# The head of a four-layer kernel: identity by way of DRAM, earlier loads, later roots

## The chip, the cores and the metric

The kernel runs on one core of a Trainium2 chip. The metric is the device time of one launch in microseconds (us). A core has five engines with a queue of instructions each: PE (TensorE, matmul), DVE (VectorE), ACT (ScalarE), POOL (GpSimd) and SP (SyncE, which here only issues DMAs). DMAs can be issued from SP, ACT and POOL.

## The reference, cut to what matters

x is 1 x 256 x 256 x 128 in float32: 65,536 tokens of 128 channels, 33.6 MB. Four layers follow, each `x = x + f(_gn(x))`, where `_gn` is a group norm over all tokens in 32 groups of 4 channels. The change lies in the first layer alone:

```python
x = x + _L0_conv_ref(_gn(x), mask, ln_w, ln_b, w_tri, w_q, w_k, w_v, w_g, b_g, w_o, b_o)

# in _L0_conv_ref, a triangle attention along rows:
mu = mean(x, axis=-1); var = mean((x - mu) ** 2, axis=-1)
xn = (x - mu) * rsqrt(var + EPS) * ln_w + ln_b
tri_bias = einsum('bijd,dh->bhij', xn, w_tri)
q, k, v = xn @ w_q, xn @ w_k, xn @ w_v          # 4 heads of 32
scores = q k^T / sqrt(32) + tri_bias + mask_bias
o = sigmoid(xn @ w_g + b_g) * (softmax(scores) @ v)
return o @ w_o + b_o
```

Two facts of it matter. The group norm needs the mean and variance of all of x before anything after it can start. And the attention adds `tri_bias` of all token pairs to every row's scores, so the per-token mean and variance, and four products with `w_tri`, are needed for all tokens before the first row of attention.

## The kernel before

The work of layer 0 is laid out in two passes over x and a loop of attention. Inside them the order of instructions on each engine is the order of the program (`tc.manual_schedule()`); the constants ahead of them are placed by a scheduler.

**Constants (lines 71 to 168).** `ident`, the 128 x 128 identity that PE's transposes use, is made on POOL by `make_identity`: a memset and an affine_select, an instruction that keeps or replaces elements by their place. Two more block constants are made on POOL with two affine_selects each: `cen16` (its tile is named f1_c, 1/16 on blocks of 16) and `gmat` (1/4 on blocks of 4, the group norm's groups). Then comes `load_library` (line 98), which loads a library of POOL functions, and some fifty DMAs of weights, all issued from POOL (`column` and `weight`, lines 102 to 112, and the lines after). `w_o` is the fifth of them. `woh` (line 432) is a scaled copy of it made on DVE; the scheduler puts it among the instructions of the first pass.

**First pass (lines 257 to 379).** x is read in 32 pieces (`NSC`) of 2048 tokens, 1 MB each, in the order `order0`. `load0(i)` issues the load of piece i from SP into one of three buffers (tag "xt"). Per piece PE transposes sixteen 128 x 128 blocks (line 360) into PSUM tiles of half a piece, of which there are three; DVE takes `bn_stats` of them (line 362); ACT copies them out as channels x tokens (line 367). The first 18 pieces go back to DRAM as `xT` from three buffers of tag "xs" (line 373); the last 14 (`HELD`) stay on chip, in tiles that the attention uses later. From the seventh piece on, one step of `folds()` (weights folded with the norms) comes with each piece. The loads:

```python
for s in range(3):
    load0(s)
mk = ...; nc.sync.dma_start(mk, mask)      # line 353
for i, s in enumerate(order0):
    ...                                    # transposes, bn_stats, copies
    load0(i + 3)
    if s not in held:
        nc.sync.dma_start(xT[...], xc)     # line 373
```

[...]

**Between the passes (lines 401 to 433)** the statistics are merged into the group norm's mean and scale, on which all that follows depends.

**Second pass (lines 436 to 602).** Per piece: ACT squares the normed piece (`p_sq`, line 450); PE multiplies the piece with `wt` (rows1, line 453) and sums the squares (squares1, line 461); DVE evacuates them to `p_tr` (line 466); PE turns them (turn1, line 474); DVE puts them into `raw` (keep1, line 478). Iteration i runs rows1(i), turn1(i-2), squares1(i-1), keep1(i-2). When all pieces of a range are in `raw`, `deviation` makes the variance on DVE (three instructions a range) and its root on ACT (line 487), and `normal`, an iteration later, the reciprocal and the scaling of the products with `w_tri` (lines 492 to 494, DVE). This comes at iterations 9, 17, 24 and 29, the second to fourth with two ranges each, and for the last four pieces after the loop. Some first work of the attention is mixed in: `first_rows` at iteration 11, `first_qk` at 26, `first_v` at 27.

**Attention and the rest (from line 606)** are not touched. DVE's statistics tiles come from the pool `stats_pool` with two buffers, used in turn by the layers.

Of the kernel before, what the change touches and what calls it, by code (L numbers as in the profile page):

```python
# [32 lines left out]
def kernel(ctx: ExitStack, tc: tile.TileContext, a: dict, out: bass.AP):  # L33
# [41 lines left out]
    make_identity(nc, ident)  # L75
# [6 lines left out]
    nc.gpsimd.memset(cen16, -1.0 / 16)  # L82
    for sign, base in ((1, 0), (-1, 15)):
        nc.gpsimd.affine_select(
            out=cen16, in_=cen16, compare_op=ALU.is_ge, fill=0.0, base=base,
            pattern=[[-16 * sign, 8], [0, 16]], channel_multiplier=sign,
        )
    cen16 = cen16.rearrange("p q c -> p (q c)")
    nc.vector.tensor_tensor(cen16, cen16, ident, ALU.add)
    gmat = const.tile([P, 32, 4], F32, name="gmat")  # L90
    nc.gpsimd.memset(gmat, 0.25)
    for sign, base in ((1, 0), (-1, 3)):
        nc.gpsimd.affine_select(
            out=gmat, in_=gmat, compare_op=ALU.is_ge, fill=0.0, base=base,
            pattern=[[-4 * sign, 32], [0, 4]], channel_multiplier=sign,
        )
# [114 lines left out]
    stats_pool = ctx.enter_context(tc.tile_pool(name="stats", bufs=2, reuse_waits="tile"))  # L211

    def new_stats(name):
        return stats_pool.tile([P, T // CK, 6], F32, name=name, tag="gn_stats")

# [41 lines left out]
    with tc.tile_pool(name="x0", bufs=1, reuse_waits="tile") as xres, tc.tile_pool(name="p0", bufs=3, reuse_waits="tile") as sb:  # L257
        tags = [("x", X_BUFS)] * 5 + [("xn", 2)] * 2 + [("rs", 1)]
        held = {s: tuple(gt_tile(f"x0_{s}_{h}", *tags[2 * s + h]) for h in range(2)) for s in range(4)}
        for s in range(4, 9):  # L260
            held[s] = att_sb.tile([P, 2, GT], F32, name=f"x0_{s}", tag="qk" if s < 6 else "vg", bufs=2 if s < 6 else 3)
            held[s] = held[s].rearrange("p a t -> p (a t)")
        for s in range(9, HELD):
            held[s] = xres.tile([P, SC], F32, name=f"x0_{s}")
        order0 = [*range(HELD + FRESH, NSC), *range(HELD, HELD + FRESH), *range(HELD)]
        with tc.tile_pool(name="p0ps", bufs=3, space=PSUM, reuse_waits="tile") as ps, tc.tile_pool(name="f0ps", bufs=2, space=PSUM, reuse_waits="tile") as fps, tc.tile_pool(name="f0", bufs=1, reuse_waits="tile") as wk, tc.manual_schedule():
            xts, loaded = {}, {}

            def load0(i):

                if i < NSC:
                    s = order0[i]
                    xts[s] = sb.tile([P, 2, 8, D], F32, name="p0_x", tag="xt")
                    nc.sync.dma_start(
                        xts[s], x_tok[s * SC : (s + 1) * SC, :].rearrange("(c p k) d -> p c k d", p=P, k=8)
                    )
# [73 lines left out]
            for s in range(3):  # L350
                load0(s)
            mk = wk.tile([P, 2, N], F32, name="mk")
            nc.sync.dma_start(mk, a["L0_conv_mask"].rearrange("b (t p) n -> p (b t) n", p=P))
            for i, s in enumerate(order0):
                xt = xts.pop(s)
                xc = held[s] if s in held else sb.tile([P, SC], F32, name="p0_xc", tag="xs")
                for c in range(2):
                    pt = ps.tile([P, 8, P], F32, name="p0_t")
                    for k in range(8):
                        nc.tensor.transpose(pt[:, k, :], xt[:, c, k, :], ident)  # L360
                    for h in range(2):
                        nc.vector.bn_stats(
                            stats0[:, i * 4 + 2 * c + h, :],
                            pt[:, 4 * h : 4 * h + 4, :].rearrange("p k n -> p (k n)"),
                        )
                    xh = xc[c] if isinstance(xc, tuple) else xc[:, c * GT : (c + 1) * GT]
                    nc.scalar.copy(
                        xh.rearrange("p (n k) -> p n k", k=8),
                        pt.rearrange("p k n -> p n k"),
                    )  # L370
                load0(i + 3)
                if s not in held:
# [62 lines left out]
        with tc.tile_pool(name="p1", bufs=3, reuse_waits="tile") as wk_sb, tc.tile_pool(name="p1ps", bufs=3, space=PSUM, reuse_waits="tile") as ps, tc.tile_pool(name="p1pt", bufs=2, space=PSUM, reuse_waits="tile") as psT, tc.tile_pool(name="p1mm", bufs=3, space=PSUM, reuse_waits="tile") as psP:  # L435
# [7 lines left out]
            with tc.manual_schedule():  # L443
# [38 lines left out]
                def deviation(lo, hi):  # L482
# [3 lines left out]
                    nc.vector.tensor_scalar(var, var, 0.0, None, ALU.max)  # L486
                    nc.scalar.activation(var, var, AF.Sqrt, bias=epst)
# [63 lines left out]
                qscale = 1.0 / float(HC) ** 0.5  # L551
                for i in range(NSC + 2):
# [12 lines left out]
                    if i == 9:  # L565
                        deviation(0, 4)
                    if i == 10:
                        normal(0, 4)
                    if i == 11:
                        first_rows()  # L570
                    if i == 17:
                        deviation(4, 8)
                        deviation(14, 21)
                    if i == 18:
                        normal(4, 8)
                        normal(14, 21)
# [6 lines left out]
                    if i == 24:  # L583
                        load_rs(1)
                        deviation(8, 12)
                        deviation(21, 25)
                    if i == 25:
                        normal(8, 12)
                        normal(21, 25)
# [5 lines left out]
                    if i == 29:  # L595
                        deviation(12, 14)
                        deviation(25, 28)
                    if i == 30:
                        normal(12, 14)
                        normal(25, 28)  # L600
                deviation(28, NSC)
                normal(28, NSC)
# [1423 lines left out]
```

## Time and profile before

| | us |
|---|---|
| median of 3 runs | 3259.66 (3257.19 to 3260.97) |
| the profiled execution | 3258.13 |
| its span, first to last instruction | 3256.4 |
| first pass with the group norm, from the start | 155 |
| second pass | 95 |
| attention, about | 1180 |

Over the span PE is busy 3052.1 us (94%), DVE 2264.2 (70%), ACT 2030.0 (62%) and POOL 1725.2 (53%). The shares differ by stage: in the first 155 us PE is busy 90.5 us, DVE 94.8, ACT 67.4 and POOL 40.7, and the DMA engines have a share of 0.96; in the second pass PE is busy 89.9 of 95 us, and the DMA share is 0.77.

In the profile's timeline a line gives start and duration in us, the engine, the line of the kernel, the operation and its operands (names with numbers left out: `p_x` is a piece of x, `p_pr`, `p_tr` and `p_pt` the second pass's products, their evacuation and their turned form), and in brackets how long the engine had been idle and what ended the wait. "issue" means that it waited for nothing that the profile shows. SPq is SP's queue, PEld PE's weight loads.

### The profile page before, as it was taken

The page shows a single profiled execution, that of the slowest core. Times are in us where ns is not written, and L with a number is a line of the kernel's source. Part 1 is how long each engine was busy: PE and PEld are TensorE (multiplying, and loading weights), DVE is VectorE, ACT ScalarE, POOL GpSimd, SP SyncE. Part 2 cuts the span into 40 slices and gives each one's busy share as a digit, 9 for nine tenths or more (in the row PEclk, how much of TensorE's full clock was granted, in tenths as well). Part 3 has the DMA queues.
Part 4 walks back from the last instruction along what each step waited for, and adds up shares of the span by engine and source line. Part 5 has one row for each costly group of instructions (what it writes and reads, how often), then busy time and mean ns, then how long its engine had stood idle before and what let it go on. Part 6 is the DMA issues. An engine that isn't in the chain of part 4 may idle for free. (4 is left out here: it accounts for less than half of the span.)

```text
span 3256.4 us, 51714 instructions
## 1 busy us (share of the span) xinstructions
PE 3052.1 (94%) x19908; PEld 1634.6 (50%) x19908; DVE 2264.2 (70%) x2617; ACT 2030.0 (62%) x2272; POOL 1725.2 (53%) x925
## 2 busy tenths in 40 slices
PE   5699999999999999996799799999999989979998
PEld 4535555555555555552533344444699933324444
DVE  5657888888888888883546455454455588858887
ACT  3577777777777777754467545444344457757776
POOL 5005777777777777760268000000255568848887
PEclk8899999999999999998899899999999999989999
DMA  9972333333333333339679677666699989986775
GB/s 353 412 299 95 107 124 112 105 125 112 105 124 113 105 123 114 105 134 392 220 305 413 238 275 306 250 253 259 262 351 353 346 316 388 389 290 195 235 231 153
DMA packets 291220, 748.13 MB, mean 230 GB/s; under 512 B 68441, under 2 KB 138731, under 8 KB 242171
## 3 DMA queue, kind: packets, MB, share of 16 engines
q1 hardware_dynamic: 282065, 731.02, 61.6%
q0 software_dynamic: 6064, 12.21, 1.0%
q8 instruction: 160, 2.62, 0.3%
q10 hardware_dynamic: 2840, 1.54, 0.2%
q14 instruction: 91, 0.75, 0.1%
HBM read 457.29 MB, written 287.38 MB: 229 GB/s over the span
## 5 line engine op out<-in xcount | busy, mean ns | idle before, releaser
L680 POOL TENSOR_TENSOR p_es<-p_e 128x1024 f32<-128x1024 f32 x256 | 603.3, 2367 | 304.7 <-ACT p_e L678 234.8
L670 DVE TENSOR_TENSOR p_e<-p_S,tri_raw 128x1024 f32<-128x1024 f32 x512 | 609.2, 1212 | 144.3 <-PE p_S L660 144.2
L678 ACT ACTIVATE p_e<-p_e,mbT 128x1024 f32<-128x1024 f32 x512 | 551.9, 1138 | 62.0 <-DVE p_e L670 62.0
L1231 PE MATMUL p_pm<-p_zn,wf 128*128 128x512 f32 x1040 | 448.7, 593 | 1.9 <-ACT p_a L1266 1.9
L645 PE MATMUL p_mm<-p_xn,w 128*128 128x512 f32 x764 | 404.7, 613 | 0.1
L1231 PEld LDWEIGHTS p_pm<-p_zn,wf 128*128 128x128 f32 x1040 | 196.8, 190 | 253.9 <-issue 246.6
L660 PE MATMUL p_S<-p_qk 32*128 32x256 f32 x4096 | 295.8, 401 | 3.3 <-DVE p_e L670 3.3
L1328 POOL MEMSET k<- 128x512 f32 x1 | 0.5, 525 | 522.4 <-PE p_pm L1231 522.4
L660 PEld LDWEIGHTS p_S<-p_qk 32*128 32x128 f32 x4096 | 186.2, 184 | 159.3 <-PE p_mm L636 91.7
L1984 PE MATMUL tp_z<-p_B,tp_at 128*128 128x256 f32 x1024 | 250.7, 388 | 0.8 <-DMA p_B<-bD 0.6
L693 PE MATMUL p_o<-p_e,p_vg 128*32 128x256 f32 x4096 | 249.2, 384 | 0.0
L627 POOL TENSOR_TENSOR p_xn<-p_xn,p_rs 128x1024 f32<-128x1024 f32 x62 | 148.8, 2400 | 182.5 <-ACT p_xn L622 97.9
L1359 POOL TENSOR_TENSOR k<-k,p_sq 128x512 f32<-128x512 f32 x128 | 163.3, 1276 | 136.0 <-ACT p_sq L1357 136.0
L1984 PEld LDWEIGHTS tp_z<-p_B,tp_at 128*128 128x128 f32 x1024 | 185.1, 190 | 21.8 <-DVE tp_at L1975 1.6
L645 PEld LDWEIGHTS p_mm<-p_xn,w 128*128 128x128 f32 x764 | 125.3, 191 | 104.1 <-issue 88.3
L1358 DVE TENSOR_TENSOR k<-tp_z,k 128x512 f32<-128x512 f32 x128 | 88.5, 692 | 127.0 <-ACT p_sq L1357 127.0
L693 PEld LDWEIGHTS p_o<-p_e,p_vg 128*32 128x32 f32 x4096 | 120.5, 110 | 110.0 <-ACT p_vg L651 41.5
L651 ACT ACTIVATE p_vg<-p_mm,bgh 128x512 f32<-128x512 f32 x128 | 88.0, 687 | 135.5 <-PE p_mm L645 135.5
L1355 ACT COPY p_K<-tp_z 128x512 f32<-128x512 f32 x128 | 75.0, 586 | 155.2 <-PE tp_z L1984 155.2
L1270 DVE SCALAR_TENSOR_TENSOR p_b<-p_pm,b2w,p_b 128x1024 f32<-128x1024 f32 x64 | 82.1, 1284 | 122.2 <-PE p_pm L1231 107.8
L636 PEld LDWEIGHTS p_mm<-w,p_xn 128*128 128x128 f32 x1016 | 134.2, 192 | 61.3 <-issue 60.6
L649 ACT ACTIVATE p_qk<-p_mm,cqkg 128x512 f32<-128x512 f32 x127 | 87.3, 687 | 122.5 <-PE p_mm L645 122.1
(394 smaller groups left out, 6068.6 us busy)
## 6 DMA issues: line engine op xcount, KB each, us to landing
p_x<-x2T SPq DMA_DIRECT2D x60, 1024.0 KB
x<-x1T SPq DMA_DIRECT2D x51, 1024.0 KB
p_x<-in_x_dram SPq DMA_DIRECT2D x32, 1024.0 KB
p_x<-xT SPq DMA_DIRECT2D x64, 512.0 KB
p_rs<-rsD SPq DMA_DIRECT2D x64, 512.0 KB
x2T<-x SPq DMA_DIRECT2D x32, 1024.0 KB
aD<-p_a SPq DMA_DIRECT2D x32, 1024.0 KB
bD<-p_b SPq DMA_DIRECT2D x32, 1024.0 KB
```

What stands on the lines that cost most here:

```text
L627: nc.gpsimd.tensor_tensor(xn, xn, groups[g]["rs"], ALU.mult)
L636: nc.tensor.matmul(pm[:, k * D : (k + 1) * D], lhsT=t["xn"][:, b * P : (b + 1) * P], rhs=wf[:, 2 * D : 3 * D], start=True, stop=True,)
L645: nc.tensor.matmul(pm, lhsT=w, rhs=t["xn"][:, cs_], start=True, stop=True)
L660: nc.tensor.matmul(Ss[h // 2][:, h % 2, u, :], lhsT=t["k"][hp, r * N + u * P : r * N + (u + 1) * P], rhs=t["q"][hp, r * N : (r + 1) * N], ...
L670: nc.vector.tensor_tensor(e[:, :, 2 * p : 2 * p + 2, :].rearrange("p u h n -> p h u n"), Ss[p], triT[:, 2 * p : 2 * p + 2, :, :], ALU.add,)
L678: nc.scalar.activation(e[:, u, :, :], e[:, u, :, :], AF.Exp, bias=mbT[:, u, i : i + 1])
L680: nc.gpsimd.tensor_tensor(es, e[:, 0, :, :], e[:, 1, :, :], ALU.add)
L693: nc.tensor.matmul(t["o"][hp, r % 2, :], lhsT=t["v"][:, r * 2 + u, hp], rhs=e[:, u, h, :], start=(u == 0), stop=(u == 1),)
L1231: nc.tensor.matmul(pm[:, c, :], lhsT=wf2[:, i, :], rhs=zns[s][:, k * CK : (k + 1) * CK], start=True, stop=True)
L1358: nc.vector.tensor_tensor(k1, pz, k1, ALU.add)
L1359: nc.gpsimd.tensor_tensor(k2, k2, sq, ALU.add)
L1984: nc.tensor.matmul(pz[:, t, :], lhsT=at[:, u, t * P : (t + 1) * P], rhs=Bc[:, u, :], start=(u == 0), stop=(u == 1))
```

## The change

- `ident` comes from a diagonal written through DRAM. DVE fills a 128 x 129 tile, `seed`, with zeros and its first column with ones; ACT's queue writes it to `diagD` in DRAM and reads the first 128 x 128 elements back in rows of 128, so that each one lands a place further on. `stats_pool` is made earlier, and `seed` takes a buffer of it.
- `cen16` and `gmat` come from `ident` on DVE: a reduction over blocks and a multiplication of its broadcast. POOL no longer has an affine_select. [...]
- Six pieces of x are asked for ahead of the mask. The fourth to sixth go into the three buffers of tag "vg", which the held pieces 6 to 8 take later; the tiles of the held pieces are therefore made when they are needed. `load0(i + 6)` follows pieces 0 to 2, nothing follows pieces 3 to 5, and `load0(i + 3)` follows the later ones.
- `deviation` is split into `variance` and `root`; root comes an iteration after variance, and normal an iteration after root. For the first range variance starts an iteration earlier, so that its normal stays where it was.
- In the order that the scheduler makes, `woh` moves on DVE from behind the sixteenth `bn_stats` of the first pass to behind the sixth.

```diff
-    make_identity(nc, ident)
+    stats_pool = ctx.enter_context(tc.tile_pool(name="stats", bufs=2, reuse_waits="tile"))
...
+    diagD = dram.tile([P, P + 1], F32, name="diagD")
+    seed = new_stats("seed").rearrange("p n s -> p (n s)")[:, 0 : P + 1]
+    nc.vector.memset(seed, 0.0)
+    nc.vector.memset(seed[:, 0:1], 1.0)
+    nc.scalar.dma_start(diagD, seed)
+    nc.scalar.dma_start(ident, diagD.rearrange("p n -> (p n)")[0 : P * P].rearrange("(p n) -> p n", n=P))
...
-    nc.gpsimd.memset(cen16, -1.0 / 16)
-    for sign, base in ((1, 0), (-1, 15)):
-        nc.gpsimd.affine_select(
-            out=cen16, in_=cen16, compare_op=ALU.is_ge, fill=0.0, base=base,
-            pattern=[[-16 * sign, 8], [0, 16]], channel_multiplier=sign,
-        )
+    gmat = const.tile([P, 32, 4], F32, name="gmat")
+    blocks = const.tile([P, 32], F32, name="blocks")
+    for m, w, value in ((cen16, 16, -1.0 / 16), (gmat, 4, 0.25)):
+        block = blocks[:, 0 : P // w]
+        nc.vector.tensor_reduce(block, ident.rearrange("p (a b) -> p a b", b=w), AX.X, ALU.add)
+        nc.vector.tensor_scalar(m, block.unsqueeze(2).to_broadcast([P, P // w, w]), value, None, ALU.mult)
...
-    gmat = const.tile([P, 32, 4], F32, name="gmat")
-    nc.gpsimd.memset(gmat, 0.25)
-    for sign, base in ((1, 0), (-1, 3)):
-        nc.gpsimd.affine_select(
-            out=gmat, in_=gmat, compare_op=ALU.is_ge, fill=0.0, base=base,
-            pattern=[[-4 * sign, 32], [0, 4]], channel_multiplier=sign,
-        )
...
                 if i < NSC:
                     s = order0[i]
-                    xts[s] = sb.tile([P, 2, 8, D], F32, name="p0_x", tag="xt")
+                    if 3 <= i < 6:
+                        xts[s] = att_sb.tile([P, 2, 8, D], F32, name="p0_x", tag="vg", bufs=3)
+                    else:
+                        xts[s] = sb.tile([P, 2, 8, D], F32, name="p0_x", tag="xt")
...
-            for s in range(3):
-                load0(s)
+            for i in range(6):
+                load0(i)
...
-                xc = held[s] if s in held else sb.tile([P, SC], F32, name="p0_xc", tag="xs")
+                xc = hold(s) if s < HELD else sb.tile([P, SC], F32, name="p0_xc", tag="xs")
...
-                load0(i + 3)
+                if i < 3:
+                    load0(i + 6)
+                elif i > 5:
+                    load0(i + 3)
...
-                def deviation(lo, hi):
+                def variance(lo, hi):
...
+                def root(lo, hi):
+                    var = rsT[:, :, 8 * lo : 8 * hi]
                     nc.scalar.activation(var, var, AF.Sqrt, bias=epst)
...
+                marks = {8: [(0, 4)], 17: [(4, 8), (14, 21)], 24: [(8, 12), (21, 25)], 29: [(12, 14), (25, 28)]}
...
+                    for at, spans_ in marks.items():
+                        for k, step in enumerate((variance, root, normal)):
+                            if i == at + k:
+                                for lo, hi in spans_:
+                                    step(lo, hi)
```

The calls of `deviation` and `normal` at fixed iterations go, and after the loop the three steps run in turn for the last range.

More of the change, by code (lines that the diff above doesn't have):

```diff
@@ L6 @@
 from concourse import library_config, mybir
-from concourse.masks import make_identity
 from concourse._compat import with_exitstack
@@ L74, with new_stats @@
     ident = const.tile([P, P], F32, name="ident")
-    make_identity(nc, ident)
+    stats_pool = ctx.enter_context(tc.tile_pool(name="stats", bufs=2, reuse_waits="tile"))
+    def new_stats(name):
+        return stats_pool.tile([P, T // CK, 6], F32, name=name, tag="gn_stats")
+    diagD = dram.tile([P, P + 1], F32, name="diagD")
[4 more added lines that the diff above has]
+    nc.scalar.dma_start(ident, diagD.rearrange("p n -> (p n)")[0 : P * P].rearrange("(p n) -> p n", n=P))
     ones = const.tile([P, P], F32, name="ones")
@@ L209, in gn_groups @@
         return mean, rstd
-    stats_pool = ctx.enter_context(tc.tile_pool(name="stats", bufs=2, reuse_waits="tile"))
-    def new_stats(name):
-        return stats_pool.tile([P, T // CK, 6], F32, name=name, tag="gn_stats")
     stats0 = new_stats("stats0")
@@ L258, with hold @@
         tags = [("x", X_BUFS)] * 5 + [("xn", 2)] * 2 + [("rs", 1)]
[L259 to L264, printed above, removed]
+        held = {}
+        def hold(s):
+            if s < 4:
+                held[s] = tuple(gt_tile(f"x0_{s}_{h}", *tags[2 * s + h]) for h in range(2))
+            elif s < 9:
+                tile_ = att_sb.tile([P, 2, GT], F32, name=f"x0_{s}", tag="qk" if s < 6 else "vg", bufs=2 if s < 6 else 3)
+                held[s] = tile_.rearrange("p a t -> p (a t)")
+            else:
+                held[s] = xres.tile([P, SC], F32, name=f"x0_{s}")
+            return held[s]
         order0 = [*range(HELD + FRESH, NSC), *range(HELD, HELD + FRESH), *range(HELD)]
@@ L272, in load0 @@
                     s = order0[i]
-                    xts[s] = sb.tile([P, 2, 8, D], F32, name="p0_x", tag="xt")
+                    if 3 <= i < 6:
+                        xts[s] = att_sb.tile([P, 2, 8, D], F32, name="p0_x", tag="vg", bufs=3)
+                    else:
+                        xts[s] = sb.tile([P, 2, 8, D], F32, name="p0_x", tag="xt")
                     nc.sync.dma_start(
@@ L564 @@
                         keep1(i - 2)
[L565 to L568, printed above, removed]
+                    for at, spans_ in marks.items():
[3 more added lines that the diff above has]
+                                    step(lo, hi)
                     if i == 11:
                         first_rows()
[L571 to L576, printed above, removed]
                     if i == 20:
@@ L584 @@
                         load_rs(1)
[L585 to L589, printed above, removed]
                     if i == 26:
@@ L594 @@
                         first_v()
[L595 to L602, printed above, removed]
+                for step in (variance, root, normal):
+                    step(28, NSC)
     stats1 = new_stats("stats1")
```

## The prediction

> **What bounds the kernel now.** The change touches the first 250 us alone, so I read the page's row of DMA shares by fortieths, then windows over that stretch, then the timeline at its two ends. The page's chain stops after one step here and says nothing. Windows (columns: length, busy us of PE, PEld, DVE, ACT, POOL with instructions, granted clock, DMA share, GB/s):
>
> ```profile
> 2.00:11.00 9.00, 0.00 (x0) 0.00 (x0) 0.00 (x0) 0.00 (x0) 0.00 (x0) 1.00 0.98 368
> 11.00:17.00 6.00, 4.22 (x24) 3.98 (x24) 4.29 (x14) 1.05 (x1) 2.16 (x7) 1.00 0.10 17
> 17.00:28.00 11.00, 5.11 (x40) 4.29 (x40) 7.34 (x13) 8.15 (x9) 4.69 (x9) 1.00 0.92 315
> 28.00:118.00 90.00, 57.08 (x312) 50.61 (x312) 49.21 (x93) 33.23 (x33) 33.35 (x64) 0.72 1.02 415
> 118.00:146.00 28.00, 21.03 (x160) 17.18 (x161) 25.94 (x42) 21.04 (x21) 0.00 (x0) 1.00 1.01 391
> ```
>
> See that from 28 us to the arrival of the last piece of x at 146 us the DMA engines are full while PE, ACT and POOL have slack: this first pass over x (32 pieces read, 18 written back) is set by bytes. DVE, at 25.94 of 28 us, is near the bound only at its end. The one place where DMA stands still is 11 to 17 us. The timeline at the head says why:
>
> ```profile
> 0.96 0.21 POOL L77 MEMSET ones<- 128x128 f32 x1
> 12.05 0.28 POOL masks.py:199 TENSOR_SCALAR_AFFINE_SELECT ident<-ident 128x128 f32<-128x128 f32 x1 [10.88 <-issue]
> ...
> 12.39 4.22 PE L360 MATMUL p_t<-ident,p_x 128*128 128x128 f32 x24 [12.39 <-POOL ident masks.py:199]
> ...
> 15.77 0.37 SPq L274 DMA_DIRECT2D p_x<-in_x_dram  x1
> ...
> 19.32 0.86 POOL L111 DMA_DIRECT2D L_conv_ln_w_sb<-in_L_conv_ln_w_dram  x1 [5.11 <-issue]
> ...
> 29.37 0.23 DVE L432 TENSOR_SCALAR woh<-L_conv_w_o_sb 128x128 f32<-128x128 f32 x1 [3.85 <-DMA L_conv_w_o_sb<-in_L_conv_w_o_dram]
> ```
>
> POOL stands 10.88 us before its first affine_select, PE waits for ident until 12.39, only then is an x buffer freed, and the fourth load goes out at 15.77. Three loads and the mask (3.4 MB) last to 11 us. POOL stands another 5.11 us before the first weight DMA.
>
> In the second pass (155 to 250 us) PE runs one iteration per 2.53 us; the starts of its groups of squares (L461) show where it is held. Timeline at the second range:
>
> ```profile
> 202.38 0.35 ACT L487 ACTIVATE tri_raw<-tri_raw,epst 128x64 f32<-128x64 f32 x1 [4.39 <-DVE tri_raw L486]
> ...
> 205.54 1.06 PE L461 MATMUL p_pr<-p_sq,slide 128*32 128x512 f32 x8 [0.75 <-ACT p_sq L450]
> ...
> 207.62 0.74 DVE L466 TENSOR_SCALAR p_tr<-p_pr,off 128x512 f32<-128x512 f32 x1
> ...
> 208.42 0.66 PE L474 MATMUL p_pt<-ident,p_tr 128*128 128x128 f32 x4 [0.96 <-DVE p_tr L466]
> ```
>
> ACT waits for the variance in front of its root, its next Square is late, and PE waits 0.75 us; one iteration on, PE waits for DVE, which is inside the normals.
>
> [...] The two POOL gaps, 10.88 and 5.11 us, [...] the built program has a library reload at each (library 0 ahead of the first affine_select, library 10 at load_library). [...] This stage's queue rows give the upper one: POOL's small transfers landed 4.9 to 8.3 us after issue under full load. [...]
>
> **The change, part by part.**
>
> 1. *Identity.* Removed: one memset, one affine_select and the reload of library 0. Added: two DVE memsets (0.2 and 0.06 us by their neighbours), and two dependent DMAs on ACT's queue, which is idle until 15.95 us. Memsets end near 1.6 us; an issue takes about 0.4 us (0.37 in SP's row). [...] two at 8.3 us give 19. I take 4.5 us a hop[...]: ident near 11 us. Their bytes, 0.13 MB at 0.41 MB/us, cost 0.35 us of a full DMA.
>
> 2. *Constants.* POOL loses two memsets and four affine_selects (2.1 us); DVE gains two reduces (0.18 each) and two multiplies (0.35 each), 1.1 us, between ident and the first bn_stats. Bytes hide it; were DMA not full, it would delay the pass by 1.1 us.
>
> 3. *POOL's start.* Only library 10 is reloaded, from about 1.2 us. Call this reload R: 5.1 us (its own gap) to 10.9 us (the gap under full DMA). First weight DMA at 1.2+R; w_o landed 10.05 us after the first one (29.37 − 19.32), so at 11.25+R: 16.4 to 22.1 us. This matters because woh moves forward in DVE's order, from behind 16 bn_stats to behind six, and everything on DVE queues behind its wait for w_o.
>
> 4. *Six pieces asked for first.* Three loads move ahead of the mask on SP, three more after pieces 0, 1 and 2, none after pieces 3 to 5; 32 loads as before. Six loads, mask and diagonal are 6.69 MB: DMA is busy from 2.0 to 18.3 us. Load 6 needs PE through piece 0, ident + 2.3 us, and some 1.2 us to reach the engines: no gap while ident is there by about 14 us. If DVE is stuck at woh, SP stands at the store of piece 1, behind load 7: eight loads, store 0, mask and diagonal (9.83 MB) keep DMA busy to 26.0 us. Store 1 reaches the engines some 3.5 us after w_o lands (its bn_stats 1.25, copy 1.01, issue and start). So no gap while w_o lands by 22.5 us, R below 11.2.
>
>    Gain: the hole (in windows of one us the idle shares from 10 to 18 us sum to 6.0 us), plus half of the 0.88 us missing in 17 to 28 us (0.08 of 11), minus 0.35: **6.1 us**. Everything behind hangs on the group norm at the pass's end, so it goes through to the end.
>
> 5. *Roots an iteration later.* ACT's wait for the variance goes; no instruction is added. What is late next is DVE. Its iterations 9, 17, 24 and 29 hold the four roots. Intervals of L461 above 2.53 us: at 9, 0.04 (ACT); at 17: 0.81 (ACT) and 0.94 (DVE); at 24: 0.79 (ACT); at 29: 0.52 (ACT). At 17 the two normals are 3.54 us of DVE (204.16 to 207.70) and by themselves put the next p_tr 4.29 us after the last instead of 2.53: 1.76 us, exactly the sum that ACT and DVE cost now, so nothing is won. At 24 the normals fall into the iteration of first_qk and first_v, whose 1.98 and 1.16 us of PE cover DVE: 0.79 won. At 29 they (2.1 us) now stand before the last p_tr and hold it 0.4 us: 0.1 won. Sum **0.8 us**, bounds 0 and 2.2 (all four ACT waits).
>
> Sum: 6.9 us. The profiled execution was 3258.13 us (span 3256.4 and 1.7 around it) and becomes 3251.2; the median of the runs, 3259.66, is 1.5 above it, so I forecast 3252.8.
>
> **The rivals.** 0.2% is 6.5 us, about what a measurement of this kernel can tell from no change: below 3253.1 is faster, above 3266.2 slower.
>
> - *The forecast's case*, 0.72, from 3250 to 3255.
> - *The gap closes in part*, 0.20. Either R is 11 to 17 us: the 10.88 us gap ended just after DMA ran dry at 11 us, as if full DMA slowed it, and now DMA never runs dry; the gain shrinks by R − 11.2. Or the two hops take 8.3 us each and ident comes at 19: PE is through piece 0 at 21.3, load 6 moves at 22.5, DMA was dry from 18.3, and 2 us are left. Both: 3254 to 3259. Against: R = 5.11 began with DMA idle but ended with it full.
> - *The reload starves, the kernel is slower*, 0.06. DVE stands at woh, store 1 waits, DMA is dry from 26.0 us until R + 11.25 + 3.5. Break-even at R = 18.1, slower by 0.2% from R = 24.6. At most the reload ends 5.1 us after DMA runs dry, R = 30: gain 6.9 − 18.8, 3271.6 us. Speaks for it: nothing but the end of DMA traffic precedes 12.05[...].
> - *The change doesn't do what it says*, 0.02: prefetch was hidden anyway and the pass is DVE's, not DMA's. Then only the roots count: 3258.9. DVE's 49.21 of 90 us speak against it.
>
> **How the numbers follow.** In the forecast's case (6.9 ± 1.5 with 1 us of run scatter) two in three are below 3253.1: 0.48, the rest, 0.24, within 0.2%. The partial case is within, 0.20, and the last too, 0.02. The slower case gives 0.05 slower and 0.01 within. So 0.48, 0.47, 0.05. The range 3249.0 to 3258.5 leaves out the slower case, the top of the partial one and a little at the bottom, under 2 in 10.
>
> **What would show it.** Right: windows of 11 to 17 us at full DMA share; one POOL gap instead of two; ident's readers starting at 7 to 14 us; woh before 23 us; last load landed near 140 us instead of 146; PE waiting no longer for p_sq after the second to fourth root, but still for p_tr after the second's normals. Wrong: a DMA hole at 18 us (ident late) or at 26 us (w_o late), or a last load at 144 us or later.

## The result, and the profile after

| | before | after | ratio, 95% interval |
|---|---|---|---|
| median, first comparison (18 and 18 runs) | 3261.13 us | 3256.24 us | 0.9984, 0.9978 to 0.9990 |
| second comparison (59 and 22) | 3262.86 | 3261.09 | 0.9990, 0.9983 to 0.9998 |
| third comparison (43 and 13) | 3263.54 | 3259.43 | 0.9989, 0.9980 to 0.9998 |
| profiled execution (span) | 3258.13 (3256.4) | 3257.65 (3255.9) | |

By the ratios (those of the record, which are not the quotients of the two medians) the kernel is faster by 5.2, 3.3 and 3.6 us, some 0.1 to 0.16%; 6.9 were forecast. The one pair of profiled executions differs by only 0.5 us: the kernel after leads by 2.4 us at the start of the attention and by 4.2 to 4.9 from 1460 to 2890 us, and then the last layer takes 365 us in the one profile and 369 in the other. Neither of these later stretches is touched by the change. In the fourteen profiles of the kernels told of here the stretch from the first bias of the attention to the merged statistics of the next layer's norm takes 1208.9 to 1215.5 us and the last stretch 365 to 373 us, and the profile before happens to have the longest of the one and the shortest of the other. So nothing below is read from the end of a single profile; it is read from marks inside the first 250 us, and from the times of many runs.

The windows of the first pass in the kernel after (columns: length, busy us of PE, PEld, DVE, ACT, POOL with instructions, granted clock, DMA share, GB/s):

```profile
2.00:11.00 9.00, 0.00 (x0) 0.00 (x0) 0.00 (x0) 0.00 (x0) 5.13 (x11) 1.00 0.81 287
11.00:17.00 6.00, 2.08 (x10) 2.11 (x11) 2.04 (x14) 0.00 (x0) 4.66 (x10) 1.00 1.04 385
17.00:28.00 11.00, 9.66 (x64) 8.01 (x62) 10.14 (x18) 7.26 (x7) 8.21 (x17) 1.00 1.03 398
28.00:118.00 90.00, 56.72 (x319) 50.34 (x320) 50.01 (x94) 36.05 (x36) 19.24 (x36) 0.74 1.01 404
118.00:146.00 28.00, 21.11 (x163) 18.03 (x161) 25.59 (x40) 20.25 (x20) 0.00 (x0) 0.98 0.95 350
```

The hole from 11 to 17 us is gone, as forecast: share 1.04 where it was 0.10. But two places that were full are no longer so: 2 to 11 us (0.81, was 0.98) and, in this profile, 118 to 146 us (0.95, was 1.01; two more profiles of the same kernel have 0.97 and 1.01 there). The head of the timeline:

```profile
1.37 0.71 POOL L113 DMA_DIRECT2D L_conv_ln_w_sb<-in_L_conv_ln_w_dram  x1 [0.41 <-issue]
...
6.51 0.33 ACTq L84 DMA_DIRECT2D ident<-diagD  x1
...
14.92 5.36 PE L359 MATMUL p_t<-ident,p_x 128*128 128x128 f32 x24 [14.92 <-DMA ident<-diagD]
18.60 0.37 SPq L273 DMA_DIRECT2D p_x<-in_x_dram  x1
...
21.53 0.21 DVE L434 TENSOR_SCALAR woh<-L_conv_w_o_sb 128x128 f32<-128x128 f32 x1
```

POOL's first weight DMA goes out at 1.37 us instead of 19.32, with an unexplained wait of 0.41 us where the prediction priced a reload at 5 to 11. The identity comes at 14.9, 2.5 us later than before: the first hop took from 1.36 to 6.51, the second to 14.8. Load 6 still goes out at 18.60, in time. `woh` waits for nothing.

The second range of roots (timeline):

```profile
201.72 0.39 ACT L492 ACTIVATE tri_raw<-tri_raw,epst 128x112 f32<-128x112 f32 x1 [0.40 <-DVE tri_raw L488]
...
203.32 1.06 PE L463 MATMUL p_pr<-p_sq,slide 128*32 128x512 f32 x8
...
205.85 1.07 PE L463 MATMUL p_pr<-p_sq,slide 128*32 128x512 f32 x8
...
208.75 0.75 DVE L468 TENSOR_SCALAR p_tr<-p_pr,off 128x512 f32<-128x512 f32 x1
...
209.55 0.66 PE L476 MATMUL p_pt<-ident,p_tr 128*128 128x128 f32 x4 [1.78 <-DVE p_tr L468]
```

PE no longer waits for a Square (0.75 us before), but DVE's two normals now put `p_tr` at 208.75, 4.29 us after the one at 204.46, and PE waits 1.78 us for it.

**How much of the filled hole is left.** A table made from the windows of 1 us, by adding up what DMA moved: the time at which so many MB had been moved since the start. The roots-alone kernel has before's first pass and gives a second reading of it.

| MB moved | before | roots alone | after | after, second profile | after, third |
|---|---|---|---|---|---|
| 7 | 28.3 | 27.8 | 22.3 | 22.2 | 22.2 |
| 16 | 50.0 | 49.5 | 44.3 | 44.5 | 44.6 |
| 20 | 59.7 | 59.1 | 55.7 | 56.6 | 56.0 |
| 36 | 98.5 | 97.8 | 94.2 | 94.7 | 94.6 |
| 46 | 123.0 | 123.9 | 120.9 | 121.0 | 120.4 |
| 54 | 143.2 | 145.6 | 142.1 | 142.6 | 141.0 |

The lead is 5.8 us at 7 MB, 5.3 at 16, 3.3 at 20, 3.7 at 36 and 2.7 at 46 (means of the columns). About 2 us go at 44 to 56 us and 1 us near 115 to 121. Windows of the kernel after at both places:

```profile
48.00:50.00 2.00, 2.00 (x21) 1.95 (x19) 2.00 (x4) 0.71 (x1) 0.53 (x1) 1.00 0.81 232
114.00:116.00 2.00, 1.03 (x5) 1.06 (x6) 0.88 (x2) 1.29 (x2) 0.00 (x0) 0.50 0.89 297
116.00:118.00 2.00, 2.00 (x12) 2.00 (x11) 1.05 (x2) 0.00 (x0) 0.00 (x0) 0.50 0.95 387
118.00:120.00 2.00, 2.00 (x14) 2.00 (x13) 1.57 (x4) 1.01 (x1) 0.00 (x0) 0.65 0.45 59
120.00:122.00 2.00, 1.70 (x16) 1.43 (x14) 2.00 (x4) 1.66 (x2) 0.00 (x0) 1.00 0.76 311
```

See the two columns together: at 116 to 120 us, where the DMA share falls to 0.45, PE is busy all of the time, and its granted clock (third from the end) is 0.50 until 119 us. At 48 to 50 us PE is busy too, but at full clock; what made it late there began at 40 us:

```profile
40.22 1.93 ACT L366 COPY p_xc<-p_t 128x1024 f32<-128x1024 f32 x2 [3.11 <-DMA xT<-p_xc]
41.29 1.97 PE L359 MATMUL p_t<-ident,p_x 128*128 128x128 f32 x8 [2.40 <-ACT p_xc L366]
```

ACT waits for a store to leave one of the three store buffers, and PE waits for ACT. The timeline at the second place:

```profile
114.97 5.84 PE L359 MATMUL p_t<-ident,p_x 128*128 128x128 f32 x32 [1.42 <-DMA p_x<-in_x_dram]
118.64 2.56 SPq L273 DMA_DIRECT2D p_x<-in_x_dram  x2
```

Two pieces have landed at once; PE takes 3.65 us for the first at half clock. Only then is an x buffer free, SP's next loads go out at 118.64, and DMA, with three buffers filled or being read, has had next to nothing to move since 118. That gave two theories for what the first pass lost. **Theory A**: PE frees the three x buffers too slowly. **Theory B**: the gain is all there, and single profiles scatter.

**What ends the pass.** The arrival of the last piece is not the event that the second pass waits for. In the kernel before:

```profile
145.18 3.51 DVE L179 BATCH_NORM_AGGREGATE gn_a<-stats 128x2 f32<-128x744 f32 x1
146.02 1.94 PE L360 MATMUL p_t<-ident,p_x 128*128 128x128 f32 x16 [2.25 <-DMA p_x<-in_x_dram]
148.61 2.42 DVE L362 BATCH_NORM_STATS2 stats<-p_t 128x6 f32<-128x512 f32 x4
```

DVE merges the statistics of 31 pieces (`gn_a`) before it takes those of the last one, which therefore wait on DVE until 148.61. In thirteen of the fourteen profiles the second pass begins 9.81 to 9.84 us after `gn_a` starts; in the roots-alone profile, where the last piece came latest, 11.00. And from 119.37 us to `gn_a` DVE stood idle for only 0.9 us in the kernel before, at 2.49 us a piece. So the last 26 us of the pass are close to DVE's bound as well as to that of DMA, and the time at which PE is given the last piece, used below, is a mark of how far DMA got; what counts for the kernel is the start of the second pass: 155.02 us before and 157.89 with the roots alone, against 153.98, 155.68 and 153.68 in the three profiles of after, 2.0 us less in the mean.

### The profile page after: what moved, and what is told of

It reads as the page before. It is cut to its first block, busy times and chain, and to the rows that moved or that the text cites. A ratio compares the mean times of both kernels' runs of the same rounds, so it can differ in the third digit from the quotient of the medians.

```text
span 3255.9 us, 51705 instructions
## 1 busy us (share of the span) xinstructions
PE 3049.4 (94%) x19908; PEld 1631.7 (50%) x19908; DVE 2265.3 (70%) x2623; ACT 2030.4 (62%) x2272; POOL 1722.0 (53%) x917
```

## The experiments

All edits to the kernel after are shown against it. Lead times are against the columns above; "second pass" is the time from the second start of a group of squares to the first bias of the attention, 88.02 us before and 87.02, 87.02 and 87.03 in three profiles of after.

### The three parts alone

**Loads alone** (only the diff's hunks from `held = {}` to `load0(i + 3)`, in the kernel before).

> The kernel before with the six early loads alone: the identity and the constants stay on POOL, the roots stay where they were. Theory A (the first pass gives most of it back: what DMA makes up before 107 us is lost again at 107 to 122 us, where PE at half clock needs 3.65 us a piece and DMA 2.56): DMA busy from 11 to 17 us, the store of the 18th piece some 4 us earlier than 103.2, but the last piece freed by PE only 1 to 2 us earlier than 146.0 us; time 1 to 2 us below before. Theory B (the prediction's: the hole of 6 us is won through to the end of the pass, and the 1.0 us of the one profile is scatter): the last piece 5 to 6 us earlier, time 5 to 6 us below before. Both: since ident is there at 12.4 us from POOL here, and came at 14.9 us through DRAM, the loads without the identity give no less than the whole change did in this pass, unless DVE stands at woh for w_o (29 us).

Measured: 3260.71 us, ratio 0.9992 (0.9984 to 0.9999), 2.1 us below before. DMA was full from 11 to 17 us and the pass was ahead by 7.8 us at 7 MB and 6.8 at 16, more than with the whole change; but at 36 MB it led by only 0.3, PE was given the last piece at 146.26 us, and the second pass began at 156.65. Some 2 us of that lead go at 40 to 48 us, as with the whole change, and 4.4 between 79 and 97 us, most of it at 82 to 88. The window, and PE's line ahead of it:

```profile
82.00:88.00 6.00, 6.00 (x34) 5.54 (x35) 3.59 (x8) 1.92 (x2) 0.00 (x0) 0.69 0.69 244
```

```profile
78.42 0.58 PE L332 MATMUL f_pb<-L_conv_ln_in_b_sb,w 128*128 128x1 f32 x2 [1.26 <-DMA w<-in_L_conv_Wgo_dram]
...
81.57 0.58 PE L332 MATMUL f_pb<-L_conv_ln_o_b_sb,w 128*128 128x1 f32 x2 [2.57 <-DMA w<-in_L_conv_Wlo_dram]
82.02 5.61 PE L369 MATMUL p_t<-ident,p_x 128*128 128x128 f32 x32
...
85.70 0.39 SPq L283 DMA_DIRECT2D p_x<-in_x_dram  x1
```

PE stands in a fold for weights that POOL, which began at 22.29 us, has only just delivered; behind it two pieces wait, at half clock the first buffer comes free at 85.70, and DMA is dry. The time fits A. The last piece came no earlier than the 146.02 us of before, and the store of the 18th piece at 103.33 us instead of the 99 expected, so the place of the loss is another than either theory named: the faster pass runs into its own weights.

**Identity alone** (only the hunks from `make_identity` to `load_library`).

> The kernel before with the identity through DRAM and the constants on VectorE alone: three loads first as before, roots as before. Theory A and B alike: the hole in DMA begins at 11 us and ends when ident has landed, PE is through the first piece and the fourth load has gone out; the second hop ends soon after DMA runs dry, so ident lands at 11 to 13 us, and the hole stays 4 to 6 us long, part of it filled with POOL's weights; time within 2 us of before (0 to -2). The prediction's rival (a reload of library 10 alone takes 5 to 11 us): first weight DMA at 6 to 12 us; against it, that the reload costs nothing when this library was left loaded by the launch before: first weight DMA at 1.4 us as in the kernel after.

Measured: 3263.94, ratio 1.0004 (0.9996 to 1.0012): no difference, as expected. First weight DMA at 1.37 us, so the reload is as cheap here. The identity landed at 14.4, later than the 11 to 13 expected, and the hole moved to 14 to 20 us:

```profile
10.00:14.00 4.00, 0.00 (x0) 0.00 (x0) 0.00 (x0) 0.00 (x0) 3.52 (x7) 1.00 1.03 363
14.00:20.00 6.00, 5.21 (x24) 4.98 (x24) 4.77 (x18) 2.13 (x2) 5.21 (x12) 1.00 0.17 29
```

**Roots alone** (only `deviation`, `marks` and the loop).

> The kernel before with the later roots alone. The prediction's working: the second pass is 0.8 us shorter (0 at the second range, 0.79 at the third, 0.1 at the fourth). The one profile of the kernel after: 1.3 us shorter (0, 0.79 and 0.52), the fourth range's normals giving back 0.3. Here with an untouched first pass: intervals of the squares 2.52 and 4.29 at the second range, 2.53 at the fourth; from the first rows matmul of the second pass to the first bias of the attention 93.0 us instead of 94.4. Time 0.8 to 1.3 us below before; a rival (the root's delay costs ACT's later Squares what it saves, as a wait of PE for p_sq one iteration on) gives 0.

Measured: 3261.81, ratio 0.9992 (0.9984 to 1.0000). The second pass is 87.02 us, 1.00 shorter than before, and the same to 0.01 us in every profile with this edit: at the second range 2.52 and 4.29, at the fourth 2.53. The terms: 0.05 at the first range, 0 at the second, 0.79 at the third, 0.52 at the fourth, less 0.35 by which PE waits longer for the last `p_tr`, behind the fourth's normals (1.23 us, 0.88 before). The rest of the 1.3 that the first profile showed lies in PE's first groups of the pass, which vary by about 1 us from profile to profile. The rival (0) falls.

### The kernel after again

> The kernel after, unchanged, once more. If theory A holds (PE at half clock and then DVE take back the first pass's gain), the profile shows again DMA below 0.9 at 114 to 122 us, the last piece freed by PE at 144 to 145 us and the first rows matmul of the second pass at 153.5 to 154.5 us. If the small gain of the first pass in the one profile was scatter (theory B), the last piece comes at 140 to 142 us this time and the second pass starts near 150. Later stages that the change leaves alone: a loss of 4 us between 2890 and 2953 us that was in the one profile does not come back if it was scatter. Time 3 to 7 us below before.

Measured: 3261.09, ratio 0.9990, in time no better than the loads alone beside it on the same chip (3260.71, 0.9992). DMA share 0.58 at 118 to 120 and 0.78 at 120 to 122; PE given the last piece at 145.02, second pass begun at 155.68. Theory A's numbers but for the start, a us later than it had it and later than in the profile before (155.02); B's 140 to 142 did not come. The loss between 2890 us and the end was there again (369.7 us).

> The kernel after, unchanged, for the comparison on one chip, and a third profile. Expected as in the first two: share of DMA 0.6 to 0.75 at 6 to 10 us, below 0.9 somewhere in 42 to 52 us and in 114 to 122 us, 50th MB near 131 us, last piece freed by PE at 144 to 145 us, 87.0 us from the second of the squares' starts to the first bias of the attention. Time 3 to 5 us below before.

Measured: 3259.43, ratio 0.9989. Last piece at 143.37 us, shares of 0.54 at 6 to 8, 0.75 at 42 to 44, 0.80 at 116 to 118 us; second pass begun at 153.68. So the three dips are this kernel's own, and the small first-pass gain is no accident of one profile. Part of B is true all the same, since profiles do scatter: with before's own first pass, the roots-alone profile was given its last piece at 148.94 us and not at 146.02.

### Six pieces on the way, longer

```diff
-                    if 3 <= i < 6:
+                    if i < 24 and i % 6 > 2:
                         xts[s] = att_sb.tile([P, 2, 8, D], F32, name="p0_x", tag="vg", bufs=3)
...
-                if i < 3:
+                if i < 21:
                     load0(i + 6)
-                elif i > 5:
+                elif i > 23:
                     load0(i + 3)
```

> The kernel after, with the three borrowed x buffers kept in turn until piece 23: six pieces of x stay on the way instead of three from piece 9 on (the fourth to sixth held pieces that use these buffers are formed from piece 24 on). Theory A' (what the first pass makes up in front it loses where PE, at half clock or held by a fold, frees the three x buffers too slowly, at 42 to 52 us and at 114 to 122 us): with six on the way the DMA share stays above 0.9 at both places; the pass's 36th MB is moved at 94 us as in the kernel after (94.2, 94.7), and the 50th at 128 to 129 us (after 130.8, 131.0; before 132.7); the last piece freed by PE at 141 to 143 us instead of 144 to 145; 2 to 3 us faster than the kernel after, 6 to 7 us below before. Rival (the lost time is the DMA's own, packets that interleave badly, or DVE with 2.5 us a piece sets the end of the pass): shares stay low or the last piece comes at 144 to 146 us as before, no time won over the kernel after.

Measured: 3254.54, ratio 0.9967 (0.9955 to 0.9979): by the ratio 10.8 us below before (6.9 to 14.7; the medians differ by 8.6), more than expected. Windows:

```profile
42.00:52.00 10.00, 8.29 (x39) 7.88 (x39) 4.89 (x9) 3.38 (x4) 6.62 (x14) 0.50 1.02 406
114.00:122.00 8.00, 3.26 (x27) 2.73 (x26) 5.15 (x9) 5.24 (x6) 0.00 (x0) 1.00 1.02 416
122.00:126.00 4.00, 4.00 (x24) 3.64 (x24) 2.59 (x4) 1.18 (x2) 0.00 (x0) 0.64 0.46 134
```

Both places are full; at the first of them PE runs at half clock throughout, and with six buffers that no longer matters. The hole moved to 122 to 126 us, where three buffers serve again. 36th MB at 92.4, 50th at 128.9, last piece at 142.31: theory A's range, and the rival falls. The next run takes the second hole away too:

```diff
-                    if 3 <= i < 6:
+                    if i in (27, 28):
+                        xts[s] = xres.tile([P, 2, 8, D], F32, name="p0_x", tag=f"h{i - 15}")
+                    elif i < 24 and i % 6 > 2:
...
-                if i < 3:
+                if i < 23:
                     load0(i + 6)
-                elif i > 5:
-                    load0(i + 3)
+                elif i > 23:
+                    load0(i + 5)
...
-                held[s] = xres.tile([P, SC], F32, name=f"x0_{s}")
+                held[s] = xres.tile([P, SC], F32, name=f"x0_{s}", tag=f"h{s}")
```

> The kernel after, with six pieces of x on the way to the end of the pass: the borrowed buffers as in the run with six pieces until 23, then pieces 27 and 28 in the buffers that hold the last two held pieces later. Theory A' : the dip of 2.2 us that moved to 122 to 127 us with three buffers from piece 24 on disappears too; 50th MB at 127 us (six until 23: 128.9; after 130.8 and 131.0), last piece freed by PE at 140 to 142 us (142.3; after 144.2 and 145.0), then DVE with 2.5 us a piece may hold it. Time 2 to 5 us below the kernel after that is run beside it. Rival: DVE or the DMA's own rate sets the end, last piece at 142 us or later, no gain over the run with six until 23.

Measured: 3254.23, ratio 0.9972 (0.9964 to 0.9981), 5.2 us below the kernel after of the same chip. Share 1.03 at 122 to 126 us, 50th MB at 126.2, last piece at 140.82: as theory A has it. In time it is no better than six until 23. The last piece comes 1.5 us sooner, but the second pass begins only 0.7 us sooner (151.78, was 152.49): DVE now works for 17.7 us without a break up to `gn_a` and sets the end.

### PE's work doubled on four pieces

```diff
                     for k in range(8):
                         nc.tensor.transpose(pt[:, k, :], xt[:, c, k, :], ident)
+                    if 16 < i < 21:
+                        for k in range(8):
+                            nc.tensor.transpose(pt[:, k, :], xt[:, c, k, :], ident)
```

> The kernel after, with the transposes of pieces 17 to 20 of the first pass done twice into the same PSUM tile (the second overwrites the first): four pieces with 7.3 us of PE at half clock or 3.65 us at full clock. It tests the clock's part in the dip at 114 to 122 us. Theory A (PE at half clock is what lets DMA run dry there): PE [...] is granted the full clock before 110 us, the pieces behind take 1.9 us instead of 3.65, DMA keeps above 0.9 at 114 to 122 us and the 46th MB comes 1 to 2 us earlier than 120.9. Rival (it is the number of buffers whatever the clock, or the doubled work itself holds the pass): the dip stays or grows, 46th MB at 121 us or later, time the same as or above the kernel after.

Measured: 3255.62, ratio 0.9981 (0.9974 to 0.9988). The median is 3.8 us below that of the kernel after on the same chip although PE does more, but the intervals of the two ratios overlap (0.9980 to 0.9998 there), so the times alone do not tell the two apart. Windows, and a piece in the timeline:

```profile
114.00:116.00 2.00, 1.06 (x10) 1.09 (x11) 0.86 (x2) 1.24 (x2) 0.00 (x0) 1.00 0.95 303
116.00:118.00 2.00, 1.43 (x14) 1.23 (x12) 1.96 (x4) 0.57 (x1) 0.00 (x0) 1.00 1.04 410
118.00:120.00 2.00, 1.63 (x14) 1.20 (x13) 1.99 (x4) 1.52 (x3) 0.00 (x0) 1.00 1.00 311
```

```profile
114.94 1.94 PE L359 MATMUL p_t<-ident,p_x 128*128 128x128 f32 x16 [1.41 <-DMA p_x<-in_x_dram]
117.44 2.14 PE L359 MATMUL p_t<-ident,p_x 128*128 128x128 f32 x16 [0.57 <-DMA p_x<-in_x_dram]
```

The clock is full, a piece takes 1.94 us instead of 3.65, DMA stays busy, the 46th MB comes at 119.3 us (120.4 to 121.0 in the kernel after), and the second pass begins at 152.37 us (153.68 to 155.68). So, by this one profile, the half clock has a part in the hole at 114 to 122 us, beside the three buffers. It is not all of it: in the third profile of the kernel after the clock is full from 115 us on, and DMA still loses 0.9 us between 114 and 121, against 2.0 and some 1.4 in the first two. The moment of the change differs between the profiles: in the first one of the kernel after PE is busy 5.41 us of the 9 from 106 to 115, in turns of 3.65 us at most, and the clock stays at 0.50 until 119; with the doubled pieces it is 1.00 from 99 us on. What sets that moment was not shown.

### POOL's start

One edit holds all weight DMAs back until the identity is there:

```diff
     nc.gpsimd.load_library(library_config.all_libraries[10])
+    gate = const.tile([P, 1], F32, name="gate")
+    nc.gpsimd.tensor_copy(gate, ident[:, 0:1])
```

> The kernel after, with one POOL copy of a column of the identity ahead of the weight DMAs, so that none of them is issued before the identity is there. Theory W (POOL's small transfers make the dip of DMA to 0.62 and 0.69 at 6 to 10 us, 1.3 us, and delay the hops): share above 0.9 at 6 to 10 us and the identity before 13 us instead of 14.9. Rival D (the diagonal's own two transfers make the dip): the dip stays, 0.6 to 0.7. Both: weights from 13 to 15 us on, w_o some 10 us later at 23 to 25; DVE stands at woh if that keeps its place behind six bn_stats, and DMA gets a hole near 26 us of up to 3 us, as the prediction worked out (break at 22.5 us). Time between that of the kernel after and 3 us more.

Measured: 3252.94, ratio 0.9966 (0.9955 to 0.9977). Windows and timeline:

```profile
6.00:8.00 2.00, 0.00 (x0) 0.00 (x0) 0.00 (x0) 0.00 (x0) 0.00 (x0) 1.00 1.03 426
8.00:10.00 2.00, 0.00 (x0) 0.00 (x0) 0.00 (x0) 0.00 (x0) 0.00 (x0) 1.00 1.03 410
```

```profile
13.37 4.55 PE L361 MATMUL p_t<-ident,p_x 128*128 128x128 f32 x24 [13.37 <-DMA ident<-diagD]
13.47 0.72 POOL L115 DMA_DIRECT2D L_conv_ln_w_sb<-in_L_conv_ln_w_dram  x1
```

The dip at 6 to 10 us is gone with the weights, and the diagonal's own transfers are still there: theory W. The identity comes 1.5 us sooner (13.3, just above the 13 expected), and the feared block at `woh` did not come: w_o had landed by 20.9 us and DMA had no hole at 26. By the ratios it lies 6 to 8 us below the kernel after (0.9966 against 0.9984 to 0.9990), which did not run on this chip, where no gain over it was expected and the dip is worth 1.3. This profile, the slowest of seven executions (3259.05), was given its last piece at 145.40, its second pass began at 154.31, as in the kernel after, and it does not show where the rest comes from. The last comparison below, where both kernels ran on one chip, does not find such a gain for the gate. That stays open.

Two more take the reload apart. One leaves the other library loaded for the next launch:

```diff
                 q_half(s - 1, 1)
+                if s == NR:
+                    left = pbs[s - 1][:, 0, 0:32]
+                    nc.gpsimd.affine_select(
+                        out=left, in_=left, compare_op=ALU.is_ge, fill=0.0, base=0, pattern=[[-1, 32]],
+                        channel_multiplier=1,
+                    )
```

> The kernel after, with one affine_select behind POOL's last addition at the program's end, which leaves the other library loaded for the next launch. Theory L (a reload of the library that is loaded already costs nothing; the launch before leaves library 10): now the first weight DMA comes at 5 to 13 us instead of 1.37, w_o lands 10 us later, woh stands at it. Rival (library 10 is loaded in no visible time whatever was there before; the 5.11 and 10.88 us of before are the price of the other library or of an affine_select's first call): first weight DMA at 1.4 us again. The end of the program grows by what the reload there takes behind POOL's last addition, 0 to 11 us, so the total time may be longer in either case.

```profile
8.76 0.86 POOL L113 DMA_DIRECT2D L_conv_ln_w_sb<-in_L_conv_ln_w_dram  x1 [7.75 <-issue]
```

The start of the program is the same as after's, only what the launch before left behind is another, and POOL stands 7.75 us instead of 0.41. Theory L is shown, its rival falls. Time 3259.59, ratio 0.9991 (0.9984 to 0.9997): no slower than the kernel after, so 7 us at POOL's start are worth nothing that these runs can tell. (With the weights later, the identity came at 13.1 us here, too.)

The other brings both reloads back:

```diff
-    nc.gpsimd.load_library(library_config.all_libraries[10])
+    with tc.manual_schedule():
+        dummy = const.tile([P, 32], F32, name="dummy")
+        nc.gpsimd.memset(dummy, 0.0)
+        nc.gpsimd.affine_select(
+            out=dummy, in_=dummy, compare_op=ALU.is_ge, fill=0.0, base=0, pattern=[[-1, 32]], channel_multiplier=1,
+        )
+        nc.gpsimd.load_library(library_config.all_libraries[10])
```

> The kernel after, with one small affine_select on POOL between the memset of ones and the load of library 10: the identity still comes through DRAM and the constants from VectorE, but POOL makes both reloads again before its weights (one weight DMA goes out ahead of them; woh goes to where it stood before, behind 18 bn_stats). Theory P (what the identity's part is worth is POOL's earlier start alone): second weight DMA at 17 to 23 us; PE waits for the late weights in the folds near 75 to 82 us as in the kernel with the loads alone, DMA runs dry there for 2 to 3 us, and the 36th MB is moved at 97 to 98 us (loads alone 97.9, after 94.2 and 94.7); time as the loads and the roots together, 1 to 3 us above the kernel after. Rival (the weights come early enough either way): 36th MB at 94 to 95 us, time as the kernel after.

```profile
14.64 0.46 POOL L103 TENSOR_SCALAR_AFFINE_SELECT dummy<-dummy 128x32 f32<-128x32 f32 x1 [12.54 <-issue]
21.51 0.74 POOL L119 DMA_DIRECT2D L_conv_ln_b_sb<-in_L_conv_ln_b_dram  x1 [6.41 <-issue]
```

Half of theory P holds: PE waits for weights in the folds up to 80.40 us, DMA falls to 0.73 at 82 to 88 us, and the 36th MB comes at 96.3 (97 to 98 expected). But the time, 3256.82, ratio 0.9981 (0.9971 to 0.9990), is not above the kernel after's, where 1 to 3 us more were expected, and the second pass begins at 154.78 us, between the 153.68 and 155.68 of after. The likely reading is that what early weights save at 84 us, they cost at 6 to 10 us and by a later identity (13.5 us here); no run isolates it.

### The two best edits together

Six pieces through, and the gate.

> Both edits in the kernel after: six pieces of x on the way to the end of the pass, and POOL's weight DMAs behind a copy of a column of the identity. If the two gains are separate (the dip at 6 to 10 us, about 1.3 us and an identity 1.5 us earlier; the dry DMA at 42 to 52 and 114 to 122 us), the 4th MB is moved at 12.6 us, the 50th at 125 to 126 us, and the last piece comes at 139 to 141 us: 1.3 us below six through alone, 4 to 6 us below the kernel after. Rival (what the gate wins is lost at woh or at the folds, because the weights come 12 us later): as six through alone or above it.

```profile
2.00:11.00 9.00, 0.00 (x0) 0.00 (x0) 0.00 (x0) 0.00 (x0) 0.00 (x0) 1.00 0.99 378
11.00:17.00 6.00, 3.60 (x17) 3.64 (x18) 3.29 (x15) 0.25 (x1) 3.69 (x8) 1.00 1.04 410
...
118.00:146.00 28.00, 16.90 (x131) 13.90 (x130) 25.72 (x42) 18.61 (x20) 0.00 (x0) 0.95 1.03 414
```

Measured: 3252.08, ratio 0.9970 (0.9960 to 0.9981): 9.8 us (6.2 to 13) below before, and 7.4 below the kernel after by the medians of one chip. No window of 2 us from 4 to 146 us has a share under 0.94; 50th MB at 124.8, last piece given to PE at 137.70 us, second pass begun at 148.64, 3.1 us before six through alone. In the profiles the two gains are separate and add; this one is the fastest of its eight executions. In time the gate's 3 us on top of six through are not resolved (0.9970 against 0.9972). This version is faster than both kernels. Whether six buffers in the kernel before, without the change, would win as much was not run.

## Why the prediction was right, and where its steps were not

The direction was right, and half to three quarters of the forecast gain came (3.3 to 5.2 of 6.9 us). The measured median, 3256.24, lies 3.4 us above the forecast of 3252.8 and inside its range; 1.5 us of that are the kernel before, which was itself slower in this comparison (3261.13) than in the three runs that the forecast started from. It is partly luck that the range held: the medians of the second and third comparison, 3261.09 and 3259.43, lie above its end of 3258.5. The number is that of the rival "the gap closes in part" (3254 to 3259), for neither of the reasons given there. By its steps:

1. *Identity.* Forecast near 11 us, upper bound 19. It came at 14.9, 15.2 and 15.3. The hop was mis-sized: 5.2 us for the first and 8.3 for the second instead of 4.5 each, which was the author's estimate and lay below what any row of POOL's transfers took at the head of the profile before (4.8 us and more from issue to landing). POOL's own transfers, sent earlier by the same change, are part of it: without them the second hop took 6.4. The margin (14 us by the prediction) was overrun by 1 us without a hole behind it, and that was luck: with the dip at 6 to 10 us only 5 of the 6.7 MB asked for first had been moved by 17.2 us, so that one error covered the other.
2. *Constants* on DVE cost nothing visible, as forecast: the second and third pair of bn_stats wait for PE there, 0.41 us each.
3. *POOL's start.* R was bounded at 5.1 to 10.9 us, and was 0.4. The step that failed is "only library 10 is reloaded": it was still loaded from the launch before (7.75 us instead of 0.41 where that launch ended with an affine_select), and the gaps of the kernel before, 10.88 and 5.11 us, were the price of changing to affine_select's library and back in each launch (12.54 and 6.41 where one affine_select was put back). The rivals that hung on R fell with it; the low weight of the slower one was the author's estimate. In the run where R was 7.75, inside the bounds, the time could not be told from that of the kernel after.
4. *Loads.* The hole closed, and the lead of 6 us is there at 7 MB. What failed is **"so it goes through to the end"**: 6.1 us became 2.7 at 46 MB. The prediction took a full DMA share before as proof that bytes alone set the pass. They did only as long as three buffers sufficed: the pass that was ahead met PE at half clock, waits for its own stores, and folds. With six buffers the share stays full at 42 to 52 and 114 to 122 us, and the kernel is 5.2 us faster on one chip; at the second place a faster clock does it too, in one profile. And the pass hangs at its end on DVE, which the prediction saw near its bound there (25.94 of 28 us) and left out of the sum: what is lost before 119 us DVE, at 2.49 us a piece, can hardly make up. The price of POOL's early transfers, 1.3 us of DMA at 6 to 10 us, was missing in the sum too.
5. *Roots.* 0.8 forecast, 1.00 measured, and the second range's exchange of ACT's wait for DVE's (4.29 us) came out to the hundredth. The fourth range was under-sized: 0.52 won less 0.35, where the prediction wrote 0.1. (Its own terms, 0.79 and 0.1, make 0.9, not 0.8.)

Of "what would show it": full share at 11 to 17 us, one POOL gap (even none), woh before 23 us, and the waits at the roots were right; ident's readers began just after the 14 us stated. The last load at 144 us, which the prediction had named as a sign that it would be wrong, did come, and it marked just the step that failed. With the terms as measured, 2.7 us of the first pass at 46 MB, or 2.0 by the start of the second pass, and 1.0 of the second make 3.0 to 3.7 us; the three comparisons give 5.2, 3.3 and 3.6. That agrees in size, and no more: the two profiles with the first pass of before begin the second pass 2.9 us apart.

The case for "no change, prefetch hidden anyway" was nearer than it looked, in its number and in part in its reason: the pass as a whole was not DVE's, but its last 26 us were close to it, and more than half of the prefetch was lost on the way.

## What to carry to other kernels

In this kernel a filled hole at the head of a DMA-bound pass was kept only when the buffers behind it were deep enough (with three, a lead of 5.8 us at 7 MB was 2.7 at 46; with six, the DMA share stayed at 1.02 at both places where it had fallen): follow the bytes moved against time, not the share alone, look at the granted clock and the waits of the engine that frees the buffers, and find the instruction whose start fixes the start of the next stage. A move that starts a queue earlier also starts its small transfers earlier, beside the one transfer that everything waits for (here the DMA share fell to 0.62 at 6 to 8 us, and the identity's second hop took 8.3 us instead of 6.4); ask which of the two is needed first. And before pricing a reload of a library, ask what the launch before left loaded (here 0.41 us or 7.75).

## What the runs showed of the hardware

- POOL's wait between `ones` and the first weight DMA, with `load_library` between them, was 0.41 us in the kernel after, where the launch before had left the same library loaded, and 7.75 us where the launch before ended with an affine_select. An affine_select put back ahead of `load_library` waited 12.54 us (under full DMA), and the weight DMAs behind `load_library` 6.41. In the kernel before and the runs with the loads and the roots alone the first affine_select waited 10.88, 10.64 and 10.32 us, and the weight DMAs behind `load_library` 5.11, 8.30 (with the early loads, under full DMA) and 5.11.
- In all seven profiles where POOL's column transfers (128 elements of 4 bytes) start at 1.37 us, the share of all DMA engines falls to 0.54 to 0.72 at 6 to 8 us, while six loads of 1 MB (three with the identity alone) are queued; sent from 8.8 us on, they had a dip behind them at 14 to 16 us (0.52), and sent from 21.5 us on one at 27 to 28 us (0.56); sent from 13.5 us on, in two profiles, none. Why they disturb in one place and not in the other was not found.
- PE that was busy 5.41 us of 9 (106 to 115 us in the kernel after), with no wait longer than 2.2 us, stayed at half clock from 106 to 119 us; with the work of four pieces doubled the clock was full from 99 us on, and a piece took 1.94 us instead of 3.65.
